# Two attention layers in one kernel: another layout and order for the beginning and for the seam between the layers

## The chip, the cores and the metric

The kernel runs on one core of a Trainium2 chip. A core has five engines that work in parallel, each through its own instructions in order: TensorE (matmuls; "PE" in the profile, its weight loads "PEld"), VectorE ("DVE"), ScalarE ("ACT"), GpSimd ("POOL") and SyncE ("SP"), whose queue issues the transfers between device memory and the core. Engines wait for each other through semaphores. The metric is the device time of one execution in microseconds (us); less is better.

## The reference

x has the shape 128 x 64 x 768 (128 graphs of 64 nodes), adj is 128 x 64 x 64 and boolean; all values are f32. Layer 0 is a graph attention with 12 heads of 64, layer 1 a masked self-attention with 6 heads of 128. Each is added to its input and normalised over the last axis.

```python
# layer 0, heads a, graph b
h = einsum('bnd,ade->bane', x, W)
th = tanh(h)
attn = th @ w_src + swapaxes(th @ w_dst, 2, 3)
attn = where(attn >= 0, attn, 0.2 * attn)
attn = softmax(where(~adj, -999.0, attn))
feat = elu(concat_heads(attn @ h + b))
gate = sigmoid(x @ H_w.T + H_b)
x = layernorm(x + gate * feat + (1 - gate) * x)
# layer 1
q, k, v = heads(x @ Wq + bq), heads(x @ Wk + bk), heads(x @ Wv + bv)
probs = softmax(q @ k.T / sqrt(128) + where(adj, 0, -9e15))
x = layernorm(x + concat_heads(probs @ v) @ Wf + bf)
```

## The kernel before

The 8192 rows of x are 64 tiles of 128 rows (two graphs each), taken in 32 pairs, p = 0 to 31. `phase_a` does layer 0 for every pair and the product with W_v of layer 1 as well; `phase_b` does the rest of layer 1 in 16 groups of two pairs. Most products are fast matrix multiplications in Strassen's manner: fewer block products, paid for by sums of weight blocks (once) and of activation blocks (for each pair).

**Products of phase_a.** For pairs 2 to 30, HG is one stream of 15 steps that makes h and the gate's input together (`start_hg`, matmuls at L428). It reads the pair's transposed tiles T, eleven block sums S (`block_sum` on POOL, L668), and weight blocks and their sums in `whg` (`weight15_sum`, L331). Each step is two f32 matmuls, shown as four records, and ends in evictions: a block's first one by DVE (L746, L748: with the bias H_b) and ScalarE (L751), later ones by DVE (L757). Three PSUM chains take turns, so a step on a chain waits until the eviction before it on that chain is done. Pairs 0 and 1 use plain products: `plain` (L686) for h of pair 0 from the raw W, `plain_blocks` (L700) for h of pair 1, `plain_g` (L715, evicted on DVE at L724) for both gates, through four PSUM buffers. Pair 31 does W and G one after the other. V is a product of 7 steps (L373) which needs the normalised rows turned (`x1T`) and four `x1_sums` (`token_sums` on POOL, L456); ScalarE keeps partial results (`snap`, L655), DVE adds them (L774), and SP writes v out (L775).

**A tile's attention in phase_a** (class Tile0). Tanh (L792); products with w_dst and w_src on POOL (L796, L804) and their sums on DVE (L799, L808); dst goes out and comes back broadcast over SP (`dst_out` L814, `dst_in` L822). Then `add` on ScalarE (L846), `mask` and `top` on DVE (L853, L857), `exp` on ScalarE (L862), `scale` with a reciprocal on DVE and a product on POOL (L870, L872), `probs` (transposes on TensorE, L883, copied by ScalarE, L888), `aggregate` (L901, which also needs the half rows that `exchange` brings over SP, L832 and L833), `elu` (L923 on DVE, L930 on ScalarE), `mix1` and `mix2` (L935 to L945 on DVE), `norm1` (L495 to L506 on DVE, L507 to L512 on POOL), `norm2` (L516 on ScalarE), `spill` (L962, SP). In a pair one tile is the "lead", the other the "tail".

**What sets the order.** Nothing is moved by a compiler. Every piece of work is put into a list with a step number by `at(step, f)`; `run` issues them by rising step, and each engine executes its own part of that list in order. The step is the pair's base O[p] (0, 12, 34, 56, then every 22; 672 for pair 31) plus the table A_LEAD, A_TAIL or A_PAIR, plus a correction in MOVED with the key (pair, table, name, index), where -1 is pair 31, -2 pair 30. The steps have no unit of time: they only order the work. BEGIN holds the steps of the work that occurs once at the start, SEAM those of the work for `phase_b` that is done before `phase_a` ends: loads of Wq and Wk (L320), their sums (L331), the first four group sums (`group_sum`, L480), the load of the first four tiles for layer 1 (`load_T4`, L485).

**The beginning.** x's first tiles, W, then the six row blocks of H_w are loaded. TensorE turns x's first two tiles (L649) and H_w's row blocks (`hw_blocks`, L602); ScalarE copies the turned blocks into `whg` and, for five slots, once more into `kept_at` (L604, L608), because the weight sums overwrite those slots while `plain_g` still reads them. ScalarE also spreads W into `whg` (`spread_w`, L575). H_w's rows and the kept blocks stand in the buffer `w2_all`, which later holds the seven slots of W_v: four loaded (`weight_plain`, L341) and three sums, of twelve instructions (`weight_sums`, L337, on POOL). A load or a sum of W_v must wait for whatever still reads its place.

**The seam.** `phase_b` starts with q's stream, for which ScalarE first copies four blocks (`dup`, L1472) into a buffer that lies where buffers of `phase_a` were.

## Time and profile before

| | |
|---|---|
| median of 3 runs | 2800.06 us (2797.17 to 2802.81) |
| the profiled execution's own time | 2796.68 us |
| its span, first to last instruction | 2794.9 us |
| mean granted TensorE clock | 0.995 |
| TensorE busy | 2754.2 us, 99% of the span |
| VectorE busy | 1924.3 us, 69% |
| ScalarE busy | 1140.0 us, 41% |
| GpSimd busy | 1500.9 us, 54% |

A row of a timeline gives the start and the duration in us, the engine, the line, the operation, what it writes and reads, and in brackets how long the engine was idle before it and which instruction or transfer ended that. In a window's row stand the stretch, its length, TensorE's busy time with the number of matmuls, the granted clock (1.00 is full), the share of time in which the transfer engines were busy, and GB/s. A wait is put down to the releaser that came last by this profile.

### The profile page before, as it was taken

Reading aid. Unit: us, or ns where it says so; the run is one execution under the profiler, and the core shown is the slowest. Engines: PE = TensorE matmul, PEld = TensorE weight load, DVE = VectorE, ACT = ScalarE, POOL = GpSimd, SP = SyncE. Lnnn points to the kernel's source line nnn. Section 1 sums busy time; section 2 is a strip of 40 time slices with the busy share of each in tenths; the row PEclk is TensorE's granted clock in tenths of the full one; section 3 lists DMA queues with packets and bytes.
Section 4 is the critical chain, followed back from the end, with each engine's and each line's share of the span. In section 5 each row is a group of like instructions: output and inputs, shape, how many; then the busy total and the mean of one; then the engine's idle time right before and its main releaser. Section 6 shows DMA issues by size and latency. Waiting matters only on the chain.

```text
span 2794.9 us, 50230 instructions
## 1 busy us (share of the span) xinstructions
PE 2754.2 (99%) x17364; PEld 1940.4 (69%) x17364; DVE 1924.3 (69%) x4086; ACT 1140.0 (41%) x3625; POOL 1500.9 (54%) x1791
## 2 busy tenths in 40 slices
PE   8999999999999999999799999999999999999998
PEld 7545545555555555455578888888888888888887
DVE  4888888888888888888765555556555556555556
ACT  4566565666665655656622211122211222211223
POOL 1656556555565565565446555446455446455455
PEclk9999999999999999999999999999999999999999
DMA  5444454454454444544542322333222323222332
GB/s 148 137 142 141 135 151 131 134 152 136 134 150 132 143 140 137 151 130 135 165 162 58 97 98 84 99 95 100 94 97 78 109 81 114 91 97 75 114 108 74
DMA packets 424924, 331.97 MB, mean 119 GB/s; under 512 B 292832, under 2 KB 370400, under 8 KB 424672
## 3 DMA queue, kind: packets, MB, share of 16 engines
q1 hardware_dynamic: 424384, 328.38, 38.4%
q8 instruction: 138, 2.26, 0.3%
q14 instruction: 114, 0.93, 0.1%
q10 hardware_dynamic: 288, 0.39, 0.0%
HBM read 203.20 MB, written 112.85 MB: 113 GB/s over the span
## 4 chain that ended last, share of the span: by engine, by line
PE 94%; DVE 2%; POOL 1%; DMA 1%; ACT 1%; issue 1%; SPq 0%; POOLq 0%; DVEq 0%; ACTq 0%
PE X L428 71%; PE X L373 14%; PE pa L901 2%; PE pb L1361 2%; PE pb L1249 2%; PE pa L883 1%; PE X L715 1%; PE X L700 1%; PE X L686 0%; DMA w<-in_L_gnn_Wv_dram 0%; DMA xb<-xT_d 0%; DMA hgp<-in_L_gnn_W_dram 0%; POOL Sc L1195 0%; ACT s L862 0%; DVE w L331 0%
## 5 line engine op out<-in xcount | busy, mean ns | idle before, releaser
L428 PE MATMUL X<-S,w 128*128 128x256 f32 x2752 | 634.3, 381 | 0.0
L428 PE MATMUL X<-w,S 128*128 128x512 f32 (+1 forms) x1364 | 598.8, 583 | 10.8 <-POOL S L668 7.6
L428 PEld LDWEIGHTS X<-S,w 128*128 128x128 f32 x2752 | 521.1, 190 | 72.0
L428 PEld LDWEIGHTS X<-w,S 128*128 128x128 f32 x1364 | 254.8, 191 | 290.4 <-issue 241.5
L1227 DVE TENSOR_TENSOR xs<-xs,X 128x256 f32<-128x256 f32 x512 | 210.0, 419 | 175.3 <-PE X L428 166.4
L872 POOL TENSOR_TENSOR s<-s,rs 128x384 f32<-128x384 f32 x128 | 107.1, 838 | 366.2 <-DVE rs L870 356.3
L428 PE MATMUL X<-w,Sc 128*128 128x256 f32 x1280 | 294.6, 381 | 0.4 <-DVE xs L1227 0.4
L1210 DVE TENSOR_TENSOR k<-k,X 128x256 f32<-128x256 f32 x320 | 133.6, 421 | 210.6 <-PE X L428 162.7
L373 PE MATMUL X<-w,S 128*128 128x384 f32 x768 | 271.0, 490 | 1.6 <-POOL S L456 1.4
L428 PEld LDWEIGHTS X<-w,Sc 128*128 128x128 f32 x1280 | 241.4, 190 | 34.8 <-DVE xs L1227 1.7
L862 ACT ACTIVATE s<-s,nmx 128x64 f32<-128x64 f32 x768 | 254.8, 336 | 5.3 <-DVE nmx L857 5.3
L428 PE MATMUL X<-xb,w 128*128 128x256 f32 x1024 | 253.3, 380 | 0.8 <-ACT q L1205 0.8
L1210 DVE TENSOR_TENSOR q<-q,X 128x256 f32<-128x256 f32 x320 | 133.9, 419 | 164.4 <-PE X L428 125.1
L516 ACT ACTIVATE xs<-xs,shift,rstd 128x768 f32<-128x768 f32 x62 | 63.5, 1025 | 436.9 <-POOL shift L512 429.5
L1205 ACT ACTIVATE k<-X,bk_c 128x256 f32<-128x256 f32 x192 | 91.0, 474 | 331.7 <-PE X L428 326.9
L428 PE MATMUL X<-w,T 128*128 128x512 f32 (+1 forms) x496 | 221.8, 579 | 2.0 <-DVE hgp L757 2.0
L428 PEld LDWEIGHTS X<-xb,w 128*128 128x128 f32 x1024 | 194.9, 190 | 27.9 <-ACT q L1205 1.2
L846 ACT ACTIVATE s<-s,src 128x64 f32<-128x64 f32 x768 | 196.6, 338 | 36.2 <-DMA s<-dst_d 29.2
L757 DVE TENSOR_TENSOR hgp<-hgp,X 128x512 f32<-128x512 f32 (+1 forms) x235 | 150.7, 652 | 80.8 <-PE X L428 66.8
L1205 ACT ACTIVATE q<-X,bq_c 128x256 f32<-128x256 f32 x192 | 90.9, 474 | 276.8 <-PE X L428 276.8
L373 PEld LDWEIGHTS X<-w,S 128*128 128x128 f32 x768 | 141.0, 190 | 90.2 <-POOL S L456 1.6
L373 PE MATMUL X<-w,T 128*128 128x384 f32 x576 | 198.5, 490 | 0.6 <-DVE T L634 0.3
(144 smaller groups left out, 4662.9 us busy)
## 6 DMA issues: line engine op xcount, KB each, us to landing
xb<-in_x_dram SPq DMA_DIRECT2D x64, 384.0 KB
s<-dst_d SPq DMA_DIRECT2D x128, 192.0 KB
x_d<-xb SPq DMA_DIRECT2D x64, 384.0 KB
xT_d<-T SPq DMA_DIRECT2D x64, 384.0 KB
v_d<-v SPq DMA_DIRECT2D x128, 192.0 KB
xb<-xT_d SPq DMA_DIRECT2D x32, 768.0 KB
xb<-v_d SPq DMA_DIRECT2D x256, 96.0 KB
xs<-x_d SPq DMA_DIRECT2D x64, 384.0 KB
```

Source lines behind the costliest of these rows:

```text
L373: nc.tensor.matmul(o, self.lhsT(i, c), rhs, start=first and c == 0, stop=last and c == CH - 1, skip_group_check=True,)
L428: nc.tensor.matmul(ps, self.lhsT(r, slot, c), self.rhs(r, slot, c), start=start and c == 0, stop=stop and c == 1, skip_group_check=True,)
L516: nc.scalar.activation(r, r, AF.Identity, bias=shift, scale=rstd)
L757: nc.vector.tensor_tensor(o, o, view(ps), ALU.add if positive else ALU.subtract)
L846: nc.scalar.activation(self.s[:, a], self.s[:, a], AF.Prelu, bias=self.src[:, a : a + 1], alpha=LEAKY_ALPHA,)
L862: nc.scalar.activation(self.s[:, a], self.s[:, a], AF.Exp, bias=self.nmx[:, a : a + 1], accum_out=self.sm[:, a : a + 1],)
L872: nc.gpsimd.tensor_tensor(t, t, rs[:, :, None].to_broadcast([P, A // 2, S]), ALU.mult)
L901: nc.tensor.matmul(self.pos[h2][own, j, :], self.pt[rws, j, own], rhs, start=True, stop=True,)
L1205: nc.scalar.activation(o[:, b], ps, AF.Identity, bias=bias[:, hd : hd + 1], scale=1.0 if positive else -1.0)
L1210: nc.vector.tensor_tensor(o[:, b], o[:, b], ps, ALU.add if positive else ALU.subtract)
L1227: nc.vector.tensor_tensor(o, o, ps, ALU.add if positive else ALU.subtract)
L1249: nc.tensor.matmul(pc[own, q, i, j, :], qT[:, b, q, own], kT[:, b, q, own], start=True, stop=True,)
```

## The change

The places of buffers: H_w's six rows and the five kept blocks stand elsewhere in `w2_all` (one row goes into the buffer `pt`), such that no loaded slot of W_v lies on a kept block. The four `snap` buffers become one tile `snaps` with four slices; pair 2's transposed tiles are put there in place of two of the four T buffers.

The engines: each of the 14 sums of `whg`, the 12 of W_v, the 14 of Wq, the first 9 of Wk and the first 4 group sums has an entry that says DVE (0) or POOL (1). Before, those of W_v were POOL's and all others DVE's. Now POOL has two of `whg`'s and DVE four of W_v's; at the seam POOL has six of Wq's, five of Wk's and one group sum.

The order: BEGIN, SEAM, V_MOVED and many entries of MOVED for pairs 0 to 4 and 28 to 31 have other values. Steps before and after, for what the prediction speaks of:

| work | before | after |
|---|---|---|
| pair 2: loads for transposes | 18.55, 23.03 | 11.10, 11.14 |
| pair 2: transposes (DVE) | 28.93, 29.81 | 19.93, 20.81 |
| pair 2: S (POOL) | 30.90 to 38.35 | 20.95 to 29.85 |
| pair 0: norm1 of its second tile | 33.69 | 33.69 |
| W_v loads (SP) | 30.99 to 34.31 | 16.34 to 18.64 |
| W_v sums | 34.44 to 47 | 33 to 41.8 |
| pair 0: exchange of the first tile (SP) | 18.92 | 18.24 |
| pair 1: src_sum of its lead (DVE) | 30.79 | 30.90 |
| pair 1: last plain_g | 30.91 | 30.40 |
| pair 2: HG | 34 to 48 | 34 to 48 |
| pair 30: add of the lead (two halves) | 671.96, 674.33 | 670.38, 673.66 |
| pair 30: mask of the lead | 675.53 | 673.95 |
| pair 30: norm1 of the lead | 686.89 | 688.49 |
| pair 29: x1_sums 0 and 1 | 687.91, 688.18 | 687.91, 688.18 |
| pair 30: probs of the tail | 689.58 | 688.19 |
| pair 31: exchange of the lead | 694.98 | 692.91 |
| pair 31: x1T1, x1T0 | 709.15, 712.45 | 707.53, 710.06 |
| load_T4 for layer 1 | 713.88 | 710.11 |
| pair 31: V | 716 to 722 | 717.5 to 723.5 |

`phase_b` is unchanged; in it the probabilities are turned by transfers and a DVE transpose (`probs_out`, `probs_turn`), before and after.

```diff
 V_MOVED = {
-    -3: 2, 0: 0.5, -1: -1.0, -2: -3,
+    -3: 2, 0: 0.5, -1: 0.5, -2: -3,
 }
 SEAM = {
-    "wq": (15.2, 19.05, 21.41, 19.73, 15.24, 15.81), "wk": (23.61, 26.84, 27.25, 27.56, 31.16, 29.25),
-    "wq_sums": (43.53, 43.53, 43.53, 43.53, 44.94, 45.97, 46.03, 46.1, 46.64, 46.71, 48.03, 48.48, 51.7, 53.88),
-    "x_sums": (46.57, 48.69, 49.6, 55.88),
-    "wk_sums": (51.23, 51.23, 51.93, 52.46, 53.21, 53.21, 54.94, 54.94, 55.54), "x1T": 41.88,
+    "wq": (15.2, 20.88, 20.96, 19.74, 19.3, 19.87), "wk": (23.61, 27.31, 27.72, 28.03, 33.3, 30.87),
+    "wq_sums": (43.53, 43.53, 43.53, 43.53, 44.94, 45.97, 46.03, 46.1, 46.64, 46.71, 48.03, 48.48, 50.82, 53.0),
+    "x_sums": (47.3, 49.42, 52.14, 57.17),
+    "wk_sums": (51.23, 51.79, 51.93, 52.46, 53.21, 53.21, 54.49, 54.49, 55.09), "x1T": 38.11,
+    "q_on": (0, 0, 1, 1, 1, 0, 0, 0, 1, 0, 1, 1, 0, 0), "x_on": (0, 1, 0, 0),
+    "k_on": (1, 1, 0, 1, 1, 0, 1, 0, 0),
 }
 BEGIN = {
-    "x1_turn": 2.3, "hw": (6.84, 8.48, 10.12, 12.38, 13.26, 14.39),
-    "spread": (1.46, -1.26, -4.37, -2.42, -6.85, -5.31), "h0": (1.02, 3.49, 5.33, 6.0),
-    "h1": (8.78, 10.35, 11.68, 13.08, 14.59, 15.89), "g0": (16.99, 17.87, 19.06, 19.8, 19.94, 21.07),
-    "g1": (24, 26.46, 26.7, 28, 30.14, 30.91),
-    "sums": (16, 16.4, 16.8, 17.2, 17.6, 18, 18.96, 19.36, 19.76, 20.16, 20.63, 21.03, 21.19, 22.66),
-    "wv": (31, 30.99, 34.31, 32.04), "v_sums": (34.44, 37, 38, 40.19, 39.85, 40.46, 41.6, 42.47, 44, 45, 46, 47),
+    "x1_turn": 1.91, "hw": (2.1, 5.84, 9.65, 13.05, 14.38, 15.55),
+    "spread": (2.09, -0.54, -5.23, -7.27, -11.38, -4.36), "h0": (-1.08, 0.46, 8.81, 10.41),
+    "h1": (10.74, 11.7, 12.39, 13.08, 14.59, 15.89), "g0": (18.01, 19.91, 20.08, 21.27, 21.41, 22.09),
+    "g1": (22.76, 25.22, 26.38, 26.73, 28.31, 30.4),
+    "sums": (16, 16.4, 16.56, 16.96, 17.6, 18.3, 19.26, 19.36, 19.76, 19.77, 20.24, 21.03, 22.91, 24.38),
+    "wv": (16.38, 18.07, 18.64, 16.34), "on": (0, 0, 0, 1, 0, 0, 0, 0, 1, 0, 0, 0, 0, 0),
+    "v_on": (1, 0, 1, 1, 0, 1, 1, 1, 0, 1, 1, 0),
+    "v_sums": (33, 33.8, 34.6, 35.4, 36.2, 37, 37.8, 38.6, 39.4, 40.2, 41, 41.8),
 }
@@ MOVED: the entries that the text speaks of @@
...
-    (2, "pair", "S", 0): 0.19, (2, "pair", "S", 1): 0.19, (2, "pair", "S", 2): -1.55,
-    (2, "pair", "S", 3): 0.19, (2, "pair", "S", 4): 0.19, (2, "pair", "S", 5): 0.19,
+    (2, "pair", "S", 0): -9.76, (2, "pair", "S", 1): -9.76, (2, "pair", "S", 2): -11.5,
+    (2, "pair", "S", 3): -9.76, (2, "pair", "S", 4): -9.76, (2, "pair", "S", 5): -9.76,
...
-    (2, "pair", "xT0", None): -0.24, (2, "pair", "xb_in0", None): -0.85, (2, "pair", "xb_in1", None): 2.38,
+    (2, "pair", "xT0", None): -9.24, (2, "pair", "xT1", None): -9, (2, "pair", "xb_in0", None): -8.3,
+    (2, "pair", "xb_in1", None): -9.51,
...
-    (-1, "lead", "exchange", None): 0.56, (-1, "pair", "x1T0", None): 2.75, (-1, "pair", "x1T1", None): 6.25,
+    (-1, "lead", "exchange", None): -1.51, (-1, "pair", "x1T0", None): 0.36, (-1, "pair", "x1T1", None): 4.63,
...
-    (-2, "lead", "add0", None): 0.14, (-2, "lead", "norm1", None): -0.99,
+    (-2, "lead", "add0", None): -1.44, (-2, "lead", "add1", None): -0.67, (-2, "lead", "mask", None): -1.58,
+    (-2, "lead", "norm1", None): 0.61, (-2, "tail", "probs", None): -1.39,
...
@@ -582,15 +618,16 @@
 
         def load_hrow(oc):
 
-            hrows[oc] = w2_all[:, oc * D : (oc + 1) * D]
+            o = (0, D, 2 * D, 6 * D, 9 * D)
+            hrows[oc] = k3.tile([P, D], F32, name="pt") if oc == 5 else w2_all[:, o[oc] : o[oc] + D]
             nc.sync.dma_start(hrows[oc], H_w[oc * P : (oc + 1) * P, :])
 
         KEPT = (0, 1, 4, 5, 7)
 
         def kept_at(slot):
-            t = w2_all[:, NC * D :]
             k = KEPT.index(slot)
-            return t[:, k * 512 : (k + 1) * 512].rearrange("p (c o) -> p c o", c=2)
+            o = 3 * D + k * 512 + (k == 4) * (7 * D + 384 - 3 * D - 4 * 512)
+            return w2_all[:, o : o + 512].rearrange("p (c o) -> p c o", c=2)
 
         def hw_blocks(oc):
             hrow = hrows.pop(oc)
@@ -627,9 +664,10 @@
                 nc.sync.dma_start(xp[q * 32 : (q + 1) * 32], sv[q])
             return xp
 
-        def turn(xp):
-
-            dst = k3.tile([P, NC, P], F32, name="T", bufs=4)
+        def turn(xp, dst=None):
+
+            if dst is None:
+                dst = k3.tile([P, NC, P], F32, name="T", bufs=4)
             for h in range(2):
                 nc.vector.transpose(
                     dst[:, h * CH : (h + 1) * CH, :].rearrange("p c (t i) -> p c t i", t=4),
@@ -650,8 +688,13 @@
                 nc.scalar.copy(dst[:, half * CH : (half + 1) * CH, :], ps)
             return dst
 
+        snaps = k1.tile([P, 4 * HALF], F32, name="snaps")
+        n_snap = [0]
+
         def snap(k, ps):
-            t = k1.tile([P, HALF], F32, name="snap", bufs=4)
+            n = n_snap[0] % 4
+            n_snap[0] += 1
+            t = snaps[:, n * HALF : (n + 1) * HALF]
             nc.scalar.copy(t, ps)
             return t
 
@@ -982,14 +1025,17 @@
         for k in range(NC):
             at(BEGIN["spread"][k], lambda k=k: spread_w(k))
         for n, k in enumerate(W_ORDER):
-            at(BEGIN["sums"][n], lambda k=k: weight15_sum(whg, k, nc.vector, slice(0, 512)))
+            eng = (nc.vector, nc.gpsimd)[BEGIN["on"][n]]
+            at(BEGIN["sums"][n], lambda k=k, eng=eng: weight15_sum(whg, k, eng, slice(0, 512)))
         for k, part in enumerate(((0, 0), (1, 0), (0, 1), (1, 1))):
             at(BEGIN["wv"][k], lambda part=part: weight_plain(w2, Wv, [part]))
         for c in range(CH):
             for k in range(4):
                 at(
                     BEGIN["v_sums"][4 * c + k],
-                    lambda c=c, k=k: weight_sums(lambda s: w2[:, s, c], nc.gpsimd, [k]),
+                    lambda c=c, k=k: weight_sums(
+                        lambda s: w2[:, s, c], (nc.vector, nc.gpsimd)[BEGIN["v_on"][4 * c + k]], [k]
+                    ),
                 )
 
         at(9, lambda: nc.vector.tensor_scalar_add(b_bc, b_bc, 1.0))
@@ -1028,10 +1074,11 @@
                 at(when(p, A_PAIR, "load"), lambda p=p: load(p))
 
             def xb_in(d, i):
-                d.setdefault("xp", []).append(blocks(x_t[2 * d["p"] + i]))
+                d["xb", i] = blocks(x_t[2 * d["p"] + i])
 
             def xT(d, i):
-                d.setdefault("T", []).append(turn(d["xp"][i]))
+                dst = snaps[:, i * D : (i + 1) * D].rearrange("p (c n) -> p c n", n=P) if d["p"] == 2 else None
+                d.setdefault("T", []).append(turn(d["xb", i], dst))
 
             if p:
                 for i in range(2):
@@ -1097,6 +1144,7 @@
 
 
         early_sums = {"S": {}}
+        ENG = (nc.vector, nc.gpsimd)
 
         o = O[-1]
         early = []
@@ -1111,11 +1159,11 @@
             at(o + SEAM["wk"][k], lambda k=k: load_early(1, Wk, k))
         for k in range(len(WEIGHT_SUMS)):
 
-            at(o + SEAM["wq_sums"][k], lambda k=k: weight15_sum(early[0], k, nc.vector, slice(0, P)))
+            at(o + SEAM["wq_sums"][k], lambda k=k: weight15_sum(early[0], k, ENG[SEAM["q_on"][k]], slice(0, P)))
         for k in range(4):
-            at(o + SEAM["x_sums"][k], lambda k=k: group_sum(early_sums, k, nc.vector, EARLY[k]))
+            at(o + SEAM["x_sums"][k], lambda k=k: group_sum(early_sums, k, ENG[SEAM["x_on"][k]], EARLY[k]))
         for k in range(WK_EARLY):
-            at(o + SEAM["wk_sums"][k], lambda k=k: weight15_sum(early[1], k, nc.vector, slice(0, P)))
+            at(o + SEAM["wk_sums"][k], lambda k=k: weight15_sum(early[1], k, ENG[SEAM["k_on"][k]], slice(0, P)))
         at(o + SEAM["x1T"], lambda: load_T4(0))
         run(events, O[-1] + 80)
         return *early, early_sums["S"]
```

## The prediction

> **What bounds the kernel.** I read the page's first part, then who waited for whom on TensorE, then TensorE's timeline around each stop, then windows for the clock.

> ```profile
> PE 2754.2 (99%) x17364; PEld 1940.4 (69%) x17364; DVE 1924.3 (69%) x4086; ACT 1140.0 (41%) x3625; POOL 1500.9 (54%) x1791
> ```

> The first part: TensorE idles 2794.9 − 2754.2 = 40.7 us in all. No matmul is added or removed, so only this idle time, and time at a low clock, can be won. TensorE's waits (total, times, longest):

> ```profile
> PE pa L883 <- POOL s L872: 8.1, 6, 2.2
> PE X L428 <- POOL S L668: 7.6, 4, 4.2
> PE pa L649 <- DMA xb<-in_x_dram: 5.8, 1, 5.8
> PE X L428 <- DVE hgp L757: 3.7, 3, 1.7
> ```

> The 5.8 us is the first load of x, which the change leaves alone. The rest lies in two places: near 90 us (pair 2's first HG product) and from 1335 to 1436 us (the seam). Between 142 and 1334 us TensorE has no stop. The timeline at the first place:

> ```profile
> 87.82 0.21 DVE L504 BATCH_NORM_AGGREGATE mv<-st 128x2 f32<-128x12 f32 x1
> 88.14 0.41 DVE L748 TENSOR_TENSOR xb<-hb_bc,X 128x256 f32<-128x256 f32 x1
> 88.30 0.56 POOL L507 TENSOR_TENSOR rstd<-rstd,neg_half 128x1 f32<-128x1 f32 x1 [5.63 <-DVE rstd L506]
> 89.11 1.96 PE L428 MATMUL X<-w,S 128*128 128x512 f32 x4 [1.54 <-ACT xb L751]
> 92.81 1.00 POOL L337 TENSOR_TENSOR w<-w 128x384 f32<-128x384 f32 x1 [1.66 <-DMA w<-in_L_gnn_Wv_dram]
> 95.26 6.42 PE L428 MATMUL X<-w,S 128*128 128x512 f32 x8 [4.19 <-POOL S L668]
> ```

> POOL works in order: the block sums S (L668) stand behind norm1's rstd, which waits for DVE, and behind a sum of W_v, which waits for its load. TensorE stops 1.54 us for the first HG eviction (L748, L751) and 4.19 us for S. Then it is slow; the windows (busy, clock, DMA share, GB/s):

> ```profile
> 92.00:93.00 1.00, 0.00 (x0) 1.00 0.58 169
> 95.00:96.00 1.00, 0.74 (x1) 0.50 0.33 91
> 99.00:100.00 1.00, 1.00 (x3) 0.50 0.74 229
> 101.00:102.00 1.00, 1.00 (x4) 1.00 0.65 157
> ```

> Half clock from 95.26 to 100.7 us is 5.44 us of work at half speed: 2.7 us lost. At the seam, TensorE's timeline:

> ```profile
> 1337.56 1.13 PE L428 MATMUL X<-w,S 128*128 128x256 f32 x4 [2.66 <-POOL S L668]
> 1348.89 1.13 PE L428 MATMUL X<-w,T 128*128 128x256 f32 x4 [1.58 <-DVE hgp L757]
> 1374.75 6.07 PE L373 MATMUL X<-w,S 128*128 128x384 f32 x18 [1.42 <-POOL S L456]
> 1397.21 0.90 PE L883 MATMUL pa<-ident,s 128*128 128x128 f32 x3 [2.20 <-POOL s L872]
> 1433.28 1.13 PE L428 MATMUL X<-xs,w 128*128 128x256 f32 x4 [1.71 <-ACT xs L1472]
> ```

> From 1385 to 1397 us TensorE has almost nothing but the last pair's softmax to wait for.

> **Begin, part by part.** (1) S sooner. Pair 2's transposes go from steps 28.9 and 29.8 to 19.9 and 20.8, since they land in `snaps` and need no T buffer of pair 0; their loads go from 18.6 and 23.0 to 11.1. The eleven S follow from 20.95 to 29.85, ahead of HG at 34, rstd at 33.69 and the W_v sums. On POOL this is 11 × 0.73 (L668) = 8 us in the stretch where POOL now sits idle (two waits of 11.9 and 14.0 us between 42 and 74 us). The 4.19 us and the half clock go: **−6.9 us**.

> (2) The stop ahead of it grows. DVE runs in order from the last plain_g eviction (L724, 82.46 us) through mix1, mix2 and norm1 to L748 at 88.14 us. The new order puts src_sum (L808, 0.94 long, 0.86 from start to start) and one W_v sum between them. DVE has no W_v row; its 128x256 weight sums take 0.42 and its 128x512 sums (L480) 0.69, so 0.5. The stop goes from 1.54 to 2.9 us: **+1.4 us**. [...] Row: the 2.66 us stop before 1337.56 left the clock at 1.00, while in the 4.19 us stop it fell 2.8 us in. [...] I take 0 (2.9 is nearer to 2.66 than to 4.19) and keep 2.7 for the range.

> (3) W_v loads. The four go on SP's queue from steps 31–34.3 to 16.3–18.6. Their new places hold only H_w rows whose transposes are done by then, so SP doesn't wait. Issuing all four took 3.48 us (L341). Pair 0's exchange is queued behind three, and its reader, aggregate, comes on TensorE at 47.08 + 5 plain_g × 2.62 + 0.67 = 60.9 us. Four loads took 81.87 to 92.65, 10.8 us; starting at 44.8, when dst_in is issued, all has landed by 55.6. Cost 0, with 5 us of cover; beyond it each us is one on TensorE.

> (4) Engine per weight sum. DVE loses two of fourteen (2 × 1.22 of L331 = −2.4) and gets four W_v sums later (+2.0). POOL gets the two: it has no 128x1024 row, and from 128x384 at 1.00 and 128x768 at 1.82 I extend to 2.4 each. [...] Row:

> ```profile
> 120.90 1.71 POOL L337 TENSOR_TENSOR w<-w 128x384 f32<-128x384 f32 x1
> 121.79 1.64 DVE L945 SCALAR_TENSOR_TENSOR xb<-xb 128x768 f32<-128x768 f32 x1
> ```

> Against the usual 1.00 and 0.96; the DVE instruction before took 1.30 for 0.95. So for 0.83 + 1.00 us of POOL work DVE lost 1.0 us: 0.56 per us. POOL now has about 10 us between 47 and 68 us (two weight sums 4.8, two scales 1.7, five S 3.6). [...] I take 0.3, as part of the 3.5 falls at the end where DVE waits for the last plain_g anyway: **+0.3 us**.

> (5) TensorE's new opening order (plain 0,1 before x1's transposes, three hw_blocks earlier) issues the same matmuls. The last W quarter has landed at 14.69 us (ScalarE's wait in spread_w) and is read from 15.1; the first H_w row, now read at 19.8, has some 4.4 MB to land up to it, and the first 20 us move 286 GB/s, 5.7 MB. 0; late rows would cost up to 1 us. `snaps` as one tile: in a steady pair the DVE sink ends 0.6 us before the next snap needs it, so even a wait for the whole tile would be free.

> (6) What is late next: evictions and x1's path. DVE was busy 27.0 of the 40 us from 80 to 120; 13 us idle take up a TensorE that is 5 us sooner. Other moves in pairs 1 to 4 and 28: 0, under no stop today; DVE's 248 of 300 us is the cover; bound +2.

> Begin: −6.9 + 1.4 + 0.3 = **−5.2 us**.

> **Seam.** (7) Pair 30's add and mask move ahead by about 1.5 steps, so its exps leave ScalarE sooner, behind which L751 and L757 were late: 1.58 to 0.2 us, **−1.4**. The 2.66 us before it stays: POOL's rstd still precedes the fourth S. (8) x1_sums 0 and 1 now precede norm1's rstd on POOL (0.88 wait, 0.55, two shifts), and tail probs go ahead of V: V's third step comes another 1.4 to 1.7 us sooner. These count only as far as the last softmax moves, since TensorE waits for it. Its links run back: probs 1397.21, scale, exps, add at 1386.59, normalise (L516) and its rstd at 1384.18, mix, ELU's exp at 1377.36, and ahead of that on ScalarE the snap of V's third step, at 1374.75 + 1.93. So it moves with V: I take −2.7 for (7) and (8) together, between −1.0 (other work on ScalarE, now add and gate, ahead of ELU) and −3.1. (9) The last pair's exchange leaves SP before the spill that held it; its data came at 1390.2 and the copied probabilities at 1390.3, so alone it is worth 0. (10) x1T0 moves ahead of V's last step: hides the 0.26 us wait (**−0.3**). (11) Eleven weight sums and one x sum from DVE to POOL: TensorE's stop at 1433.28 ends with the copies L1472, which follow the V output's transfer:

> ```profile
> 1430.39 1.84 DMA v_d<-v
> 1432.61 2.18 ACT xs L1472 x4
> ```

> (start, us). Neither moves against TensorE, so 0; POOL idles 22 us there.

> Seam: **−3.0 us**. Sum −8.2 on the profiled execution's 2796.68 us (span 2794.9 and 1.8 around it): 2788.5. The median is 3.4 above that execution, so **2791.9 us**.

> **Rivals.** *Half* (0.2): the clock gate takes the longer stop (+2.7) and the seam gives its low bound (+1.7): −3.8, 2796.3, within the bound. For it: half clock in three places of this trace; against: 2.66 us went free. *No effect* (0.07): TensorE reaches 116 us sooner and waits there for DVE (98% busy from 120 to 140 us), and the softmax doesn't move: 2800. Against: no DVE wait there today. *Port lock* (0.16, slower): POOL's added sums hold DVE's second port. [...] *More* (0.07): the seam's shorter stop also keeps the clock, which was half from 1388 to 1402 us with some 8 us of work in it: −4 more, 2788.

> **Numbers.** Likeliest 0.5, 2791.9 (2788 to 2795). Measurement can tell 0.2%, 5.6 us. Faster: 0.46 of the likeliest, the 0.07, and 0.05 of half: 0.58. Same: 0.04 + 0.15 + 0.06 = 0.25. Slower: 0.17. Range 2784 to 2803: it leaves out most of port lock and little below.

> **What would show it.** Right: no S wait at pair 2's HG, clock 1.00 from 93 to 100, a stop of 2.5 to 3.3 us at its fourth step; the last probs at the seam 7 to 8 us earlier in the span than 1397. Wrong: DVE's L331 at 1.6 us and more beside POOL's; stops on L724 (60 to 80 us) or new ones from 100 to 140; V waiting at 1370 as before.

## The result and the profile after

The changed kernel takes **2792.98 us** (median of 9 runs, 2791.74 to 2795.36); the kernel before takes 2799.99 us in the same comparison (median of 9, 2796.97 to 2802.81). The ratio is 0.9977, with a 95% interval of 0.9966 to 0.9987: 7.0 us less. 2791.9 had been predicted. The profiled execution took 2795.36 us (span 2792.7), the slowest of its nine, while that of the kernel before took 2796.68 (span 2794.9), less than any of the nine it is compared by. So the two traces differ by 2.2 us and the medians by 7.0, and a row-by-row comparison shows where things moved, not the whole gain.

The page of the changed kernel, first part, and TensorE's waits (total, times, longest):

```profile
PE 2754.4 (99%) x17364; PEld 1942.8 (70%) x17364; DVE 1922.5 (69%) x4076; ACT 1138.7 (41%) x3625; POOL 1514.9 (54%) x1801
```

```profile
PE pa L926 <- POOL s L915: 10.0, 4, 4.5
...
PE X L464 <- ACT xb L794: 4.0, 1, 4.0
PE X L464 <- POOL S L711: 3.6, 2, 2.7
PE X L464 <- DVE hgp L800: 2.1, 2, 1.7
```

The waits on S fell from 7.6 to 3.6 us: the one of 4.19 at pair 2 is gone. The wait for the first HG eviction, 1.54 before, is now 4.0, and those for the probabilities (L926) went from 8.1 to 10.0. TensorE's idle time is 2792.7 − 2754.4 = 38.3 us for 40.7.

At the begin, the timeline (start, us, engine, line, operation) of the changed kernel:

```profile
77.58 2.53 POOL L839 TENSOR_TENSOR w<-th,wd_bc 128x768 f32<-128x768 f32 x1
80.15 0.95 DVE L842 TENSOR_REDUCE sd<-w 128x12 f32<-128x768 f32 x1 [1.38 <-POOL w L839]
90.49 0.56 DVE L373 TENSOR_TENSOR w<-w 128x384 f32<-128x384 f32 x1
90.97 0.41 DVE L791 TENSOR_TENSOR xb<-hb_bc,X 128x256 f32<-128x256 f32 x1
91.85 7.11 PE L464 MATMUL X<-w,S 128*128 128x512 f32 x12 [3.98 <-ACT xb L794]
```

The first eviction is reached at 90.97 us (88.14 before). In its windows (length, busy, clock, DMA share, GB/s) the clock still falls behind the stop, but for 3.4 us, not 6.8:

```profile
91.00:92.00 1.00, 0.15 (x1) 1.00 0.00 0
92.00:93.00 1.00, 1.00 (x3) 0.84 0.00 0
94.00:95.00 1.00, 1.00 (x2) 0.50 0.99 365
96.00:97.00 1.00, 1.00 (x3) 0.95 0.03 3
```

At the seam, TensorE's timeline:

```profile
1334.02 1.13 PE L464 MATMUL X<-w,S 128*128 128x256 f32 x4 [2.67 <-POOL S L711]
1387.21 0.90 PE L926 MATMUL pa<-ident,s 128*128 128x128 f32 x3 [4.50 <-POOL s L915]
1394.95 0.90 PE L926 MATMUL pa<-ident,s 128*128 128x128 f32 x3 [2.12 <-POOL s L915]
1431.67 1.13 PE L464 MATMUL X<-xs,w 128*128 128x256 f32 x4 [1.71 <-ACT xs L1520]
```

The 1.58 us stop in G is gone. The stop of 1.42 us in V is 0.20, and that step runs at 1370.73 for 1374.75. But the last probabilities came only 2.3 us sooner (1394.95 for 1397.21) and pair 30's V only 0.9 (1396.99 for 1397.90). Pair 28's V, ahead of the seam, was already 3.5 us sooner (1312.47 for 1316.00), so within the seam this trace lost 2.6 us of what the begin had gained. The chain that ended last has another middle than before (start, us, what):

```profile
1372.81 3.66 DMA x_d<-xb
...
1377.82 5.95 DMA xp<-x_d
...
1383.83 6.19 DMA x_d<-xb
...
1390.08 0.60 SPq L664
...
1392.04 4.08 DMA xp<-x_d
...
1396.24 0.70 DVE T L672
```

Both tiles of pair 30's x1 go out to memory and come back, and V waits for the second. Before, this stretch ran through the last pair's exchange and softmax.

### The profile page after: what moved, and what is told of

It reads as the page before. It is cut to its first block, busy times and chain, and to the rows that moved or that the text cites. A ratio compares the mean times of both kernels' runs of the same rounds, so it can differ in the third digit from the quotient of the medians.

```text
span 2792.7 us, 50231 instructions
## 1 busy us (share of the span) xinstructions
PE 2754.4 (99%) x17364; PEld 1942.8 (70%) x17364; DVE 1922.5 (69%) x4076; ACT 1138.7 (41%) x3625; POOL 1514.9 (54%) x1801
## 4 chain that ended last, share of the span: by engine, by line
PE 95%; DVE 1%; POOL 1%; DMA 1%; ACT 0%; issue 0%; SPq 0%; POOLq 0%; DVEq 0%; ACTq 0%
PE X L464 71%; PE X L409 15%; PE pa L944 2%; PE pb L1409 2%; PE pb L1297 2%; PE pa L926 1%; PE X L743 1%; PE X L758 1%; PE X L729 1%; POOL Sc L1243 0%; DMA xp<-x_d 0%; DMA x_d<-xb 0%; DMA hgp<-in_L_gnn_W_dram 0%; POOL S L711 0%; POOL xs L1225 0%
## 5 line engine op out<-in xcount | busy, mean ns | idle before, releaser
L464 PE MATMUL X<-w,T 128*128 128x512 f32 (+1 forms) x480 | 215.1, 580 | 0.4 <-DVE hgp L800 0.4
L889 ACT ACTIVATE s<-s,src 128x64 f32<-128x64 f32 x768 | 196.5, 338 | 38.7 <-DMA s<-dst_d 34.2
```

The lines of the kernel that those rows point to most:

```text
L464: nc.tensor.matmul(ps, self.lhsT(r, slot, c), self.rhs(r, slot, c), start=start and c == 0, stop=stop and c == 1, skip_group_check=True,)
L889: nc.scalar.activation(self.s[:, a], self.s[:, a], AF.Prelu, bias=self.src[:, a : a + 1], alpha=LEAKY_ALPHA,)
```

## The experiments

In the table, *against before* is the median less the median of the kernel before in the same runs. Where the text says *against the changed kernel*, it is the difference of two entries of this column. The four places are starts in the trace: pair 2's HG, pair 0's V, pair 28's V, and the first product of the last stage. *Lost to half clock* is the sum of 1 − granted clock over windows of 1 us (2 us in the last stretch) after pair 2's HG stop, in W's stretch (1326 to 1346 us), and from 1346 to 1440 us. It is the most that half clock can have cost: in the last stretch TensorE waits for much of that time anyway.

| kernel | median, us | against before | ratio, 95% interval | HG 2 | V 0 | V 28 | last stage | lost to half clock |
|---|---|---|---|---|---|---|---|---|
| before | 2799.99 | | | 82.26 | 118.68 | 1316.00 | 1429.68 | 3.4 / 0 / 8.5 |
| changed | 2792.98 | −7.0 | 0.9977 (0.9966–0.9987) | 82.56 | 115.97 | 1312.47 | 1428.07 | 1.7 / 3.4 / 8.5 |
| begin alone | 2793.09 | −7.2 | 0.9976 (0.9965–0.9986) | 82.67 | 116.09 | 1312.29 | 1427.61 | 1.7 / 1.7 / 6.8 |
| seam alone | 2798.59 | −1.7 | 0.9995 (0.9988–1.0001) | 82.23 | 118.54 | 1315.95 | 1431.99 | 3.4 / 1.7 / 8.5 |
| S back | 2798.35 | −1.7 | 0.9994 (0.9985–1.0003) | 84.26 | 119.89 | 1316.69 | 1430.55 | 0 / 1.7 / 8.5 |
| old engines | 2795.31 | −5.0 | 0.9982 (0.9975–0.9989) | 83.84 | 117.93 | 1314.43 | 1430.08 | 1.7 / 0 / 8.5 |
| W_hg sums on DVE | 2795.71 | −5.4 | 0.9984 (0.9975–0.9993) | 83.86 | 117.81 | 1314.12 | 1429.23 | 1.7 / 3.4 / 6.8 |
| product first | 2793.21 | −7.1 | 0.9971 (0.9960–0.9983) | 82.58 | 115.65 | 1311.96 | 1427.80 | 1.7 / 1.7 / 8.5 |
| evictions first | 2792.87 | −7.2 | 0.9978 (0.9969–0.9987) | 82.61 | 116.45 | 1312.99 | 1430.70 | 3.4 / 1.7 / 10.2 |
| x1 turn later | 2792.79 | −7.3 | 0.9975 (0.9967–0.9984) | 82.37 | 115.77 | 1312.12 | 1429.18 | 1.7 / 3.4 / 8.5 |
| loads at old steps | 2798.41 | −2.7 | 0.9994 (0.9985–1.0003) | 83.37 | 118.14 | 1314.77 | 1433.29 | 3.4 / 1.7 / 10.2 |
| loads late | 2790.46 | −9.6 | 0.9969 (0.9957–0.9981) | 82.13 | 116.74 | 1313.04 | 1424.78 | 3.4 / 1.7 / 6.8 |
| PE filled | 2790.66 | −10.4 | 0.9964 (0.9950–0.9977) | 82.79 | 115.99 | 1312.20 | 1426.09 | 0 / 0 / 1.7 |
| all that helped | 2784.08 | −17.0 | 0.9940 (0.9928–0.9952) | 82.78 | 115.00 | 1311.69 | 1419.48 | 0 / 0 / 0 |

An interval is some ±3 us wide, so a difference of 2 us between two kernels is not shown by the times alone; where the text makes one, it rests on the trace, of which there is one for each kernel.

### Begin or seam

Begin alone: the changed kernel with the seam's steps and engines of the kernel before.

```diff
+MOVED = {k: v for k, v in MOVED.items() if k[0] >= 0}; MOVED.update({...before's entries for the last pairs...})
+SEAM.update({...before's steps..., "q_on": (0,) * 14, "x_on": (0,) * 4, "k_on": (0,) * 9}); V_MOVED.update({-1: -1.0})
```

> The begin of the changed kernel with the seam of the kernel before (all its steps of the last four pairs, and every early sum of attention's weights on DVE). My theory: the begin carries most of the gain, -4 to -5 us against the kernel before (2795 to 2796), because pair 2's S sums no longer stand behind the r-standard-deviation steps on POOL; in the trace no wait on S at pair 2's first HG step, a stop of about 4 us at its fourth, and pair 0's V 2 to 3 us earlier. Rival, the forecast's own split: -5.2. Rival, the seam carries it: no more than -1 here.

Seam alone: the kernel before with the changed seam.

```diff
+MOVED = {k: v for k, v in MOVED.items() if k[0] >= 0}; MOVED.update({...the change's entries for the last pairs...})
+SEAM.update({...the change's steps and engines...}); V_MOVED.update({-1: 0.5})
```

> The begin of the kernel before with the seam of the changed kernel (its steps of the last four pairs, and its engine for each early weight sum). My theory: V of pair 29 gets going about 4 us sooner, but the round trip of pair 30's x1 through memory takes most of it back before pair 30's V, so -1 to -2 us against the kernel before (2798 to 2799). Rival, the forecast: -3.0 (2797). Rival, the whole gain is the begin's: 0 +- 0.5.

Begin alone gives −7.2 us, as much as the whole change; seam alone −1.7, with an interval that reaches to no change. So the begin carries the gain (5.2 had been forecast for it, within the interval), and the seam adds nothing measurable on top of it.

### S ahead of the waits on POOL, undone

```diff
-(2, "pair", "S", 0): -9.76, ... (2, "pair", "S", 10): -10.83,
+(2, "pair", "S", 0): 0.19, ... (2, "pair", "S", 10): -0.88,
```

> The changed kernel with pair 2's eleven S sums back at the steps of the kernel before (behind the r-standard-deviation steps and among W_v's sums on POOL); all else as changed. My theory, the forecast's first step: the wait of about 4 us on S at pair 2's HG is back and the half clock behind it, +4 to +7 us against the changed kernel (2797 to 2800); pair 0's V near 118.5 us. Rival, the stop only moves: with S late, HG's fourth step comes late too, so the stop of 3.98 us on the eviction shrinks by as much as the wait on S costs, +0 to +2 (2793 to 2795). Rival, the engines: with four of W_v's twelve sums on DVE, POOL gets to S sooner than before, so the wait is 2 us at most, +1 to +3.

The expected +4 to +7 came: +5.3 us against the changed kernel, and pair 0's V 3.9 us later. TensorE's timeline of this kernel:

```profile
84.26 1.98 PE L464 MATMUL X<-w,S 128*128 128x512 f32 x4 [1.71 <-POOL S L711]
88.02 1.98 PE L464 MATMUL X<-w,S 128*128 128x512 f32 x4 [1.77 <-POOL S L711]
93.08 1.96 PE L464 MATMUL X<-w,S 128*128 128x512 f32 x4 [1.36 <-ACT xb L794]
...
98.27 1.98 PE L464 MATMUL X<-w,S 128*128 128x512 f32 x4 [0.65 <-POOL S L711]
```

The wait on S comes back in four pieces, and the stop on the eviction shrinks from 3.98 to 1.36. The order of S is what the begin's gain hangs on. But the half clock that was expected with it did not come: the stops add to 6.1 us, but none is over 1.8, and the clock stays at 1.00 from 80 to 100 us.

### Which engine does a sum

Every weight sum on its old engine, and then W_hg's two sums alone:

```diff
-"on": (0, 0, 0, 1, 0, 0, 0, 0, 1, 0, 0, 0, 0, 0), "v_on": (1, 0, 1, 1, 0, 1, 1, 1, 0, 1, 1, 0), ...
+"on": (0,) * 14, "v_on": (1,) * 12, "q_on": (0,) * 14, "x_on": (0,) * 4, "k_on": (0,) * 9
```

> The changed kernel with each weight sum on the engine that it had before (W_hg's all on DVE, W_v's all on POOL, those of the seam all on DVE), steps and places left as changed. If which engine does a sum matters little, as the row of 0.56 us lost on DVE per us of POOL work says: within 1 us of the changed kernel (2792 to 2794). [...] Rival, DVE is the late engine at the stop in pair 2's HG: the first W_v sum back on POOL takes 0.56 us off that stop, and the sums back on DVE at the seam delay evictions, in sum +1 to +2 (2794 to 2795).

```diff
-"on": (0, 0, 0, 1, 0, 0, 0, 0, 1, 0, 0, 0, 0, 0)
+"on": (0, 0, 0, 0, 0, 0, 0, 0, 0, 0, 0, 0, 0, 0)
```

> The changed kernel with W_hg's two sums that it has on POOL back on DVE, all else as changed. If the 1.3 us by which pair 2's HG came later with every sum on its old engine are these two sums (1.22 each on DVE, in the row that feeds the plain products): HG at 83.8 for 82.6, and +1.3 us against the changed kernel (2794.3). Rival, W_v's sums are what counts: HG at 82.6, within 0.5 us of the changed kernel. [...]

+2.0 and +1.6 us, with HG at 83.8 in both: by these starts it is W_hg's two sums, and the other 16 that changed engine (4 of W_v's, 12 at the seam) show nothing beyond them. DVE's timeline, changed kernel and then with the sums back:

```profile
47.05 4.75 DVE L367 TENSOR_TENSOR w<-w 128x1024 f32<-128x1024 f32 x4 [1.96 <-PE X L743]
54.74 3.63 DVE L367 TENSOR_TENSOR w<-w 128x1024 f32<-128x1024 f32 x3
58.29 0.42 DVE L767 TENSOR_TENSOR xb<-X,hb_bc 128x256 f32<-128x256 f32 x1
```

```profile
47.08 5.89 DVE L367 TENSOR_TENSOR w<-w 128x1024 f32<-128x1024 f32 x5 [1.95 <-PE X L743]
55.91 4.89 DVE L367 TENSOR_TENSOR w<-w 128x1024 f32<-128x1024 f32 x4
60.72 0.42 DVE L767 TENSOR_TENSOR xb<-X,hb_bc 128x256 f32<-128x256 f32 x1
```

With five and four sums for four and three, the same eviction comes 2.43 us later, and 1.3 of that reaches TensorE. The change has put pair 2's four turns (L672, two at a time, 1.3 us each) at 58.6 and 61.6 us, ahead of where they were (76.1 and 78.5), and with these ahead of it DVE has no room left for the two sums.

### The stop at HG's fourth step

Pair 1's destination product (L839) ahead of S 7, 6 and 9 on POOL:

```diff
-(2, "pair", "S", 6): -9.51, (2, "pair", "S", 7): -9.76, (2, "pair", "S", 9): -9.58
+(2, "pair", "S", 6): -7.58, (2, "pair", "S", 7): -7.71, (2, "pair", "S", 9): -8.35
```

> The changed kernel with three of pair 2's S sums (6, 7 and 9) put behind pair 1's product with the destination weights on POOL instead of ahead of it. My theory: that product is what DVE waits for at 80.15 (1.38 us), so the ELU, the mix and HG's first eviction all come 1.2 to 1.4 us sooner, and the stop of 3.98 us at pair 2's fourth HG step shrinks to about 2.6; against the changed kernel -1.0 to -1.4 us (2791.6 to 2792). If the stop is what drops the clock there, up to -3. Rival, DVE's own row of work sets the stop: it shrinks by less than 0.4 us, no difference in the time. Rival, the S sums come late again: a new wait on S at the seventh or eighth HG step, slower by up to 1.

The product came 2.7 us sooner, DVE no longer waited for it, and yet the stop only went from 3.98 to 3.64 us: the first rival. The second rival didn't come true. The time is the changed kernel's, within what these runs can tell. Most of the 1.38 us that the wait gave up went into two DVE instructions that met POOL's work. One, with POOL's beside it:

```profile
84.94 0.99 POOL L373 TENSOR_TENSOR w<-w 128x384 f32<-128x384 f32 x1
```

```profile
84.97 1.78 DVE L979 SCALAR_TENSOR_TENSOR xb<-xb 128x768 f32<-128x768 f32 x1
```

L979 takes 0.96 alone. The other is L987 at 75.83, 1.65 beside the product that had been moved there.

Then norm1 of pair 0 and DVE's first W_v sum behind HG's first two evictions:

```diff
-(0, "tail", "norm1", None): 0.17
+(0, "tail", "norm1", None): 1.52, (0, "tail", "norm2", None): 0.5, (0, "tail", "spill", None): 0.5
-"v_sums": (33, 33.8, 34.6, ...
+"v_sums": (33, 35.05, 34.6, ...
```

> The kernel with the destination product ahead of three S sums on POOL, and besides that pair 0's first normalisation (its statistics on DVE, its output and store) and DVE's first W_v sum put behind the first two evictions of pair 2's HG. My theory: DVE's row of work sets the stop at the fourth HG step, 1.9 us of it stand ahead of the first eviction (two statistics 1.02, aggregation 0.21, r-standard-deviation 0.15, sum 0.56), so the stop shrinks from 3.64 to about 1.7 us and the half clock behind it goes or gets shorter: -1.5 to -3.5 us against the kernel with the destination product first (2790 to 2792). Rival, the store of x1 that follows the normalisation comes late and pair 0's V waits: no gain, or +1. Rival, the clock gate doesn't answer to this stop: -1.5 to -2, with the half clock unchanged.

In this kernel W_v's second and third sums change places, so the third takes an operand that the second hasn't replaced yet, and v comes out wrong. It serves for its time alone: the instructions are the same ones. Expected was a stop of 1.7 us; it was 3.12, and the time did not move (−0.2 us). One row holds the rest:

```profile
86.88 2.55 POOL L839 TENSOR_TENSOR w<-th,wd_bc 128x768 f32<-128x768 f32 x1 [0.92 <-ACT th L835]
```

```profile
87.80 2.44 DVE L988 SCALAR_TENSOR_TENSOR xb<-xb 128x768 f32<-128x768 f32 x1
```

With POOL's r-standard-deviation out of the way, the next product (L839) came sooner and met L988: 2.44 us for 0.96.

### What holds the seam

The turn of pair 30's second x1 tile behind the last softmax's reciprocal, mask and maximum:

```diff
-(-2, "pair", "x1T1", None): 1.54
+(-2, "pair", "x1T1", None): 3.4
```

> The changed kernel with the turn of pair 30's second x1 tile on DVE, and its store on the DMA queue, put behind the reciprocal, mask and maximum of the last softmax and behind the exchange of the last pair. My theory: in the trace of the changed kernel the reciprocal of the last pair's leading tile stands behind that turn, which waits 3.59 us for its load; without it the probabilities' second half comes 3 to 4 us sooner (1383.5 for 1387.2), the exchange about 2 us; but pair 30's V waits for the other tile's turn (1396.24) all the same, so the time moves by -0.5 to 0. Rival, the last softmax sets the seam's end: -2 to -3 us (2790 to 2791). Rival, DVE is what is short there: the turn comes back later, +1.

The probabilities' second half came at 1382.60 for 1387.21, and the time stayed (−0.3 us), as expected: V still waited for the other tile, which landed at 1396.1. So the reciprocal behind the turn was a real wait, off the path.

The loads of attention's weights behind the load of x1 on SP's queue, and at the steps of the kernel before:

```diff
-"wq": (15.2, 20.88, 20.96, 19.74, 19.3, 19.87), "wk": (23.61, 27.31, 27.72, 28.03, 33.3, 30.87)
+"wq": (15.2, 27.2, 27.3, 27.4, 27.5, 27.6), "wk": (27.9, 28.2, 28.5, 28.8, 33.3, 30.87)
```

> The changed kernel with five of the six loads of attention's first weight tile and the four next ones put behind the load of pair 30's x1 on the DMA queue (1390 us and later; they are summed from 1410 on). My theory: the store of x1 took 6.19 us here and 3.4 before because these loads share the transfer engines with it; without them pair 30's V starts about 2 us sooner (1395 for 1397), -1 to -2 us (2791 to 2792). Rival, what is late is the work that feeds the store (mix and normalisation on DVE), not the store: within 0.5 of the changed kernel. Rival, the loads come too late for their sums: +1 to +3 at the start of the last stage.

```diff
-"wq": (15.2, 20.88, 20.96, 19.74, 19.3, 19.87), "wk": (23.61, 27.31, 27.72, 28.03, 33.3, 30.87)
+"wq": (15.2, 19.05, 21.41, 19.73, 15.24, 15.81), "wk": (23.61, 26.84, 27.25, 27.56, 31.16, 29.25)
```

> The changed kernel with the loads of attention's first two weight tiles back at the steps of the kernel before, all else as changed. My theory now: with the changed seam the end is set by the round trip of pair 30's x1 through memory, and it is the load steps of the change that put four of these loads beside that store and load; so back at the old steps the store takes about 3.4 us for 6.2 and pair 30's V starts 1 to 2 us sooner: -1 to -2 us against the changed kernel (2791 to 2792). Rival, any early load does it, wherever it stands before 1385: within 0.5 us of the changed kernel, and only the late loads (2790.5) help. Rival, it was the execution's clock: no difference in the trace either, store 6 us.

With late loads −2.6 us against the changed kernel, where −1 to −2 had been expected; pair 30's V starts at 1393.0, and the chain goes through the softmax again:

```profile
1391.12 0.20 DVE rs L913
...
1391.38 0.84 POOL s L915
...
1392.27 0.90 PE pa L926 x3
1393.17 3.84 PE X L409 x6
```

From pair 28's V to the last stage it takes 111.74 us, for 115.60 in the changed kernel. From 1364 to 1400 us the queue's packets took 67.9% of the transfer engines' time, for 85.1%.

The loads at their old steps were expected to help a little, and cost 4.3 us: my theory of that moment, that the change had moved these loads to a bad place, fell. The chain of that kernel:

```profile
1391.78 0.87 SPq L356
...
1392.75 0.60 SPq L664
...
1394.97 5.61 DMA xp<-x_d
...
1401.44 1.65 PE X L409 x2
```

The second Wk load (L356) now stands ahead of the load of x1 (L664) on SP and flows beside it: 5.61 us for 4.08. Measured from pair 28's V, pair 30's V comes 2.15 us later than in the changed kernel and the last stage 2.9. Pair 2's HG and pair 0's V were late in this execution too (+0.8, +2.2), long before these loads, so I take the seam's 2.9 us as the price and leave the other 1.4 to the executions. By this trace the changed steps were better than the old ones, and not late enough.

### TensorE kept busy in its stops

```diff
+        FILL = {("HG", 2, 3): 24, ("W", 31, 4): 16, ("W", 31, 5): 5, ("probs", 1): (6, 28), ("probs", 0): (14, 12)}
+        def fill(n, ps=None):
+            ps = psa.tile([P, CH, P], F32, name="pa") if n and ps is None else ps
+            for _ in range(n):
+                nc.tensor.transpose(ps[:, 0, :], ident, ident)
...
+                    fill(FILL["probs", self.i][q] if self.last else 0, ps)
...
-                    at(t0 + i * dt, lambda d=d, key=key, i=i: d[key].step(i))
+                    at(t0 + i * dt, lambda d=d, key=key, i=i, n=FILL.get((key, p, i), 0): (fill(n), d[key].step(i)))
```

> The changed kernel with transposes of the identity on PE, of no use to the result, ahead of the steps that wait: 24 at pair 2's fourth HG step, 16 and 5 in the last pair's W, and 6, 28, 14 and 12 ahead of the four halves of the last probabilities. My theory: one stop of 3 us and more is what lets the gate halve the clock, in windows of 3.4 us that lose 1.7 each; with PE kept busy the half clock after HG's stop (one or two windows) and most of that from 1386 to 1400 goes: -3 to -5 us against the changed kernel (2788 to 2790), the stops themselves unchanged. Rival, the gate doesn't count such transposes: no difference. Rival, they run past the wait and hold up what is due: +1 to +2 (2794 to 2795).

−3.4 us against the changed kernel. The windows of the changed kernel, and then of the filled one:

```profile
80.00:100.00 20.00, 16.02 (x39) 0.91 0.24 75
1326.00:1346.00 20.00, 16.39 (x59) 0.83 0.50 140
1376.00:1404.00 28.00, 16.73 (x137) 0.76 0.97 259
```

```profile
80.00:100.00 20.00, 18.45 (x76) 1.00 0.21 67
1326.00:1346.00 20.00, 18.34 (x91) 1.00 0.47 139
1376.00:1404.00 28.00, 21.56 (x198) 0.94 0.94 238
```

No half clock in the first two places and one window of it in the third: with these transposes, of no use to the result, the granted clock was 1.00, 1.00 and 0.94, for 0.91, 0.83 and 0.76. At HG it did not pay: the fourth step starts at 92.09 us, for 91.85 in the changed kernel, and pair 0's V at 115.99 for 115.97, since TensorE at full clock now waits for evictions (0.16 and 0.54 us, which were not there). The gain was at the seam: the next stop in G is at 1356.50 us for 1359.05, and pair 30's V at 1394.88 for 1396.99.

Last, the product first, the late loads and the fill (22, 16, 5, and 6, 6, 22, 12) together:

> The changed kernel with the destination product ahead of three S sums, the weight loads behind the load of pair 30's x1, and transposes of the identity in PE's waits (22 in HG, 16 and 5 in W, 6, 6, 22 and 12 in the last probabilities). If the three gains add up (-0.5 to -1.5, -2.3, -3 to -5): -6 to -8 us against the changed kernel (2785 to 2787). If the late loads already shorten the waits that the transposes fill, they add less: -4 to -5 (2788 to 2789). If transposes are late for the work behind them: 2790 or more.

−10.0 us against the changed kernel, −17.0 against the one before, more than the best case expected. In this trace no half clock is left in any of the three places, and pair 30's V starts 7.2 us sooner than in the changed kernel:

```profile
1389.45 0.55 PE L932 MATMUL pa<-ident,s 128*128 128x128 f32 x3 [0.96 <-POOL s L920]
1389.84 2.10 PE L409 MATMUL X<-w,T 128*128 128x384 f32 x6
```

The single gains add up to 6.1, so the parts seem to help each other: late loads make the softmax the last to come, and at full clock its transposes and aggregates between the waits are short (three transposes take 0.55 us, for 0.90 at half clock in the changed kernel). That is my reading; no run has the late loads and the fill without the product first. Its five runs lie within 0.5 us (2783.9 to 2784.4); the kernel before's 41 within 7.3.

## Why the prediction was right, and where only its sum was

The time was 1.1 us above the forecast and the gain 7.0 for 8.2. By the medians the two halves were off by more, with opposite signs: the begin gave 7.2 for 5.2, the seam 0 to 1.7 for 3.0. Neither is off by more than the interval, but the traces below show that the seam's mechanism failed, so that the sum came so close is in part luck.

- **(1) S sooner, −6.9.** The mechanism held: the wait of 4.19 us is gone, and undone it costs 5.3, which is steps (1) and (2) together, forecast at 5.5. One term was wrong, the 2.7 us of half clock: 1.7 us are still lost behind the stop in the changed kernel's trace.
- **(2) The stop grows to 2.9 us, clock taken as untouched.** The stop is 3.98. The working listed src_sum and the W_v sum on DVE and left out that the S sums stand ahead of pair 1's product on POOL, for which DVE waits 1.38 us, and that three two-input instructions on DVE took longer beside POOL's work (L987 1.24 us, L988 1.37 and L978 1.35, between 75.8 and 86.1 us, for 0.96). On the clock the working went by one row, 2.66 us at a clock of 1.00, and the runs show another thing at HG: behind a stop of 3.12 us or more the granted clock fell to 0.50 in each of the eleven traces that have one, the changed kernel's among them. The shortest of these stops, 3.12 us, is shorter than one window of half clock, 3.41 us (last section).
- **(3) W_v's loads at no cost, (5) the new opening order at no cost.** Right. TensorE has no wait on a load between 14 and 82 us. HG starts 0.30 us later; in that execution the first load of x came 0.27 later, and the clock's first record, from which `plain`'s matmuls start every 0.32 us (0.64 ahead of it), is at 14.17 us for 12.02. So a cost of the opening order below 1 us can't be told from these two traces.
- **(4) Engine per sum, +0.3.** Right in size, with one term missed. Pair 2's four turns moved ahead on DVE with S, 2.6 us that were not priced, and the two sums that went to POOL, 2.43 us, made room for them; with the sums back on DVE, HG starts 1.3 us later. No stop on L767 appeared between 60 and 80 us, so the rival *port lock* is out, and no run shows the port that it names. Nor does any show the 3.5 us on DVE of which the 0.3 was taken as a part: in the changed kernel's trace the two-input DVE instructions that took longer beside POOL between 47 and 68 us are L367 at 52.12 us (by 0.55), L367 at 60.14 (by 0.32) and L896 at 66.37 (by 0.17), 1.0 us together.
- **(6) Nothing late next.** Right: no new stop between 100 and 140 us, and pair 28's V is 3.5 us sooner than before, more than pair 0's 2.7.
- **(7) and (8) V's third step and the softmax with it, −2.7.** This is the step that failed, in its second half. Counted from pair 28's V, which leaves out what the begin gave, V's third step (in pair 29's V) starts 58.75 us later in the kernel before, and 55.99, 56.01 and 56.00 us later in the three traces that have the changed seam and the clock full in W (old engines, PE filled, all that helped): 2.75 sooner, as forecast. In the changed kernel's own trace it is 58.26, with two windows of half clock in W. Then it ended: "it moves with V" followed one chain of links and never asked for the second way into pair 30's V, x1's trip to memory and back. From V's third step to pair 30's V the kernel before takes 23.15 us and the changed kernel 26.26, so what the first half gained is spent there. With the loads late it is 22.44. The forecast also gave no price to these weight loads, which the change moves on SP's queue, though they ran beside that trip: from 1364 to 1400 us the queue's packets took 85.1% of the transfer engines' time, for 67.9% with the loads late. Their places alone are worth +2.9 us in the trace at the old steps and −2.6 in the median when later.
- **(9) to (11).** (9) and (11) hold: the 1.71 us stop after V's output is unchanged, and the engines at the seam show no difference. (10) holds: the 0.26 us wait is gone, though V's start as a whole moved by 0.9.
- **The signs named beforehand.** No S wait: seen. Clock at 1.00 from 93 to 100 us: not seen. A stop of 2.5 to 3.3: it was 4.0. Last probabilities 7 to 8 us earlier: 2.3. Of the signs of being wrong, one showed in part: a weight sum on DVE (1.22 us alone) took 1.77 at 52.12 us beside POOL's scale, and 1.54 at 60.14 behind POOL's weight sum. Both signs of the rival *half* came (the clock fell behind the longer stop, the seam gave its low bound or less), and only the larger gain of the begin in the medians kept the time from it.

What stays open: begin alone is 7.2 us faster by medians and 3.7 at pair 28's V by the traces. The traced execution of the kernel before lies 3.3 us below its median and shows no half clock in W, where six of the seven other traces with a stop of 2.66 us or more at this place show one window or two. That could make up part of the difference, but there is no second trace of the kernel before to show it. At the seam, the last probabilities start 12.3 us after the last pair's second add (L889, 1382.64 us), for 10.6 before; with the x1 turn later it is 11.5, and what makes the rest is open.

## What to carry to other kernels

When one input of a waiting product is made earlier, list every other input of that product, round trips through memory among them, and price what else is on their queue; the next to be late is often one of these. Count a stop of TensorE together with the clock that it can cost, which came in windows of 3.41 us here: one stop of 3.98 us was followed by such a window at 0.50, five stops of 6.1 us in all, none over 1.8, by none, and transposes of no use in the long stops took 3.4 us off the time. For DVE work with two inputs, look at what POOL does at the same moment, not at POOL's busy share: one such instruction took 2.44 us beside POOL's, for 0.96.

## What the hardware showed

**Half clock came in whole windows.** In all 14 traces here a stretch of half clock lasts 3.41 us or a multiple of it (the one that the kernel's end cuts off aside), so it took at most 1.7 us of work or a multiple (the table's last column). Single stops of 3.12 to 4.52 us at HG's fourth step were followed by one window in six traces and by two in three. W's stop of 2.66 to 2.68 us at the same place in the program was followed by none, one or two.

**DVE instructions of 128x768 with two inputs, neither in PSUM, ended 0.81 to 0.82 us after the POOL instruction that they met.** The forecast's row (POOL 120.90 + 1.71 = 122.61, DVE 121.79 + 1.64 = 123.43) was read as 0.56 us lost per us of POOL work. DVE ends 0.82 us after POOL there. In the kernel with the product first it is 86.75 against 85.93, again 0.82; in the next one 90.24 against 89.43, 0.81. In the traces of the kernel before and of the changed one, 26 of these instructions (mask, mix1 and mix2) began while a POOL instruction had more than 0.15 us to run, and each ended 0.81 or 0.82 us behind it. Alone they take 0.95 or 0.96, so what such a meeting cost was what was left of POOL's instruction, less some 0.14 us, and not a share of POOL's work: 1.48 us at most in the rows shown here (2.44 for 0.96). In the forecast's row POOL's sum, 0.997 to 1.013 us elsewhere in that trace, took 1.71; it began at 120.90, while DVE was in L944 until 121.76. An eviction, with one of its inputs in PSUM (where the kernel's matmuls write), shows nothing of this: L1227 in the trace of the kernel before took 0.40 to 0.42 us in each of its 512 instructions, 465 of which began while POOL was at work. Whether the two engines meet was a matter of the order of their work, in which the kernels here differ.
